# A transformer block on one core: how the high part of the row maxima is written

## The chip, the cores and the metric

The kernel runs on one core of a Trainium2 chip. The time is the device time in microseconds of one execution, and the number quoted is the median of several executions. TensorE (PE in the profile) multiplies, VectorE (DVE), ScalarE (ACT) and GpSimd (POOL) work on tiles of 128 partitions, and SyncE (SP) issues most of the transfers.

## What is computed

One block of a conditioned transformer, in fp32: two sequences of 2048 tokens, 512 channels, 16 heads of 32 channels, and an MLP of 2048 hidden channels. A condition vector gives shift, scale and gate for both halves.

```python
mod = jax.nn.silu(condition) @ Wada + bada
sh_a, sc_a, gt_a, sh_m, sc_m, gt_m = jnp.split(mod, 6, axis=1)
xm = _layernorm(x, g1, be1) * (1.0 + sc_a[:, None, :]) + sh_a[:, None, :]
x = x + gt_a[:, None, :] * _attention(xm, Wqkv, Wproj, bproj)
xm = _layernorm(x, g2, be2) * (1.0 + sc_m[:, None, :]) + sh_m[:, None, :]
h = jax.nn.gelu(xm @ W1 + b1, approximate=False)
x = x + gt_m[:, None, :] * (h @ W2 + b2)
```

The attention is causal and its softmax is over the keys:

```python
scores = jnp.einsum('bhqd,bhkd->bhqk', q, k) * scale
scores = jnp.where(causal, scores, -jnp.inf)
attn = jax.nn.softmax(scores, axis=-1)
```

The softmax needs, for every query, the largest of its scores. How these maxima are stored is what the change touches.

## The kernel before

**Stages.** Per sequence: layer norm and the products for queries, keys and values (`Qkv`), attention (`attention_phase`), the output projection (`project_phase`). The MLP of all tokens comes last. In the profiled execution the first sequence's attention runs from about 225 to 800 us, the second's from about 1060 to 1635 us.

**Units.** Attention is cut into units `(c, i)`: four heads `c` (`HC` = 4) and a block `i` of 512 queries, in four tiles of 128 (`TQ` = 4). A sequence has 16 units, in the order `i` = 0, 1, 2, 3 for the first four heads and 0, 2, 1, 3 for the others. A unit with block `i` looks at `i + 1` blocks of 512 keys.

**Every score is computed twice.** First with queries on the partitions, for the maxima only: `bank` (L424) multiplies one tile of queries by one block of keys into a PSUM bank `s` and VectorE takes the row maximum into a column of `mx`, with `tensor_reduce` (L441) for a full block and with a masked sum and maximum (L436, `junk`, followed by a read of its accumulator) for the block on the diagonal. There are two banks `s` (`ps_sp`, `bufs=2`); in some steps one of the `st` banks is borrowed. A bank can be written again only when VectorE has read it. Second with keys on the partitions (`scores_t`, L524): `st` is started with minus the maximum of each query (a matmul of `sel`, all -1, with `fold`), the scores are added to it, ScalarE takes the exponential into `e` (L565), GpSimd masks the diagonal tiles (L571) and adds pairs and fours of `e` tiles for the row sums (L593, `ee`), and TensorE multiplies `e` by the values into `o` and by ones into `sm`.

**From maxima to `fold`.** When the last maximum of a unit is there, `score` calls `split` (L444). `mx` has 16 rows of four heads times four tiles, with one value for each key block. If there is more than one block, L453 takes the maximum over the blocks into `m`, 128x16. Then two numbers are written for each maximum, next to each other in one of three tiles `mhl`: the high part, `m` written in the matmul's type fp32r (L455), and the low part, `m` less the high part (L456). Later `rows` (L492) lets TensorE transpose `mhl` into a bank `s` (`ps_m`) and VectorE spreads that into `fold` (L500).

**Order.** TensorE runs its matmuls in program order, as written. Scores for the maxima run up to two units ahead (`AHEAD` = 2) and are dealt out between the steps of the unit under work by planned costs: `cost` for a bank, `due` for what is to be done by a step. So there are stretches, at the end of a unit, in which every allowed score is already done. VectorE takes its instructions in the order of one queue: what stands behind a stalled one waits, whatever it needs. GpSimd does the same; in attention it has trains of eight or more additions `ee` of 128x512, and in the last stage of the queries and keys it prepares MLP weights (L911, `w`). The last unit's `ee` sums run on VectorE.

Of the kernel before, what the change touches and what calls it, by code (L numbers as in the profile page):

```python
# [12 lines left out]
ALU = mybir.AluOpType  # L13
AX = mybir.AxisListType
# [13 lines left out]
def dit_block_kernel(  # L28
# [35 lines left out]
    nc = tc.nc  # L64
# [5 lines left out]
    HC = P // HD  # L70
# [12 lines left out]
    def pool(name, bufs=1, **kw):  # L83
# [25 lines left out]
        axis=AX.XY,  # L109
        op=ALU.add,  # L110
# [7 lines left out]
    for n in range(AHEAD + 1):  # L118
        m = bp.tile([P, HC, HD], F32R, tag=f"mhl{n}", name=f"mhl{n}")
# [154 lines left out]
    class Row:  # L274
# [169 lines left out]
        def split(self, u, mx):  # L444
            nb = units[u][1] + 1
            hl = mhl[u % (AHEAD + 1)][:, :, : 2 * TQ].rearrange(
                "p h (t l) -> p h t l", l=2
            )
            if nb == 1:
                m = mx[:, :, 0]  # L450
            else:
                m = bp.tile([P, HC * TQ], F32, tag="m1", name="m1", bufs=2)
                nc.vector.tensor_reduce(m, mx, axis=AX.X, op=ALU.max)  # L453
            m = m.rearrange("p (h t) -> p h t", h=HC)
            nc.vector.tensor_copy(hl[:, :, :, 0], m)  # L455
            nc.vector.tensor_tensor(  # L456
                hl[:, :, :, 1], m, hl[:, :, :, 0].bitcast(F32), ALU.subtract
            )
# [670 lines left out]
    with ExitStack() as mlp:  # L1129
# [249 lines left out]
        for m in range(NM):  # L1379
            h = [  # L1380
                [
                    mp.tile([P, 4, MT], F32, tag="h4", name="h4", bufs=2 * FC // 4)
                    for _ in range(FC // 4)
                ]
                for _ in range(2)
            ]
# [87 lines left out]
```

## Time and profile before

| What | Value |
|---|---|
| Median of three executions | 2513.37 us (2510.52 to 2516.57) |
| Profiled execution, its time | 2510.99 us |
| Profiled execution, its span | 2509.3 us |
| Mean granted TensorE clock | 0.99 |
| L441, maxima of full blocks, 768 of them | 429.6 us in 634 from `s`, 92.2 us in 134 from `st` |
| L593 on GpSimd, pair sums `ee<-e` | 420.2 us in 336, 1287 ns each |
| L593 on GpSimd, four sums `ee<-ee` | 211.2 us in 168, 1285 ns each |
| L455 with `m`, units of two to four key blocks | 50.9 us in 24 |
| L455 with `mx`, units of one key block | 1.4 us in 8 |
| L453 | 4.8 us in 24 |

A row of a timeline gives start in us, duration in us, engine, line, operation, output and inputs with shapes, how many were merged, and in brackets how long the engine had been idle before and what ended that. A group's row ends with busy time, mean ns of one, and idle time before it. A matmul with another operand may start while the one before is still shown as running, since the ends of matmuls are modelled.

### The profile page before, as it was taken

What the parts mean: (1) busy time and instruction counts of PE and PEld (TensorE: products, weight loads), DVE (VectorE), ACT (ScalarE), POOL (GpSimd) and SP (SyncE); (2) the same over time, 40 slices, a digit from 0 to 9 for tenths busy, and PEclk for the clock granted to TensorE, in tenths of its full rate; (3) what the DMA queues carried; (4) which work ended last, traced back from release to release, by engine and by line L of the source; (5) the groups of instructions that cost most, each with busy time, mean ns of one, the idle gap of its engine ahead of it and who ended that gap; (6) DMA issues with size and microseconds to landing.
All of it is one profiled execution on the core that took longest, in us unless ns stands there. A gap on an engine that the chain in (4) does not pass through costs nothing.

```text
span 2509.3 us, 30950 instructions
## 1 busy us (share of the span) xinstructions
PE 2440.3 (97%) x10977; PEld 1178.9 (47%) x10977; DVE 1401.8 (56%) x2820; ACT 892.6 (36%) x1667; POOL 978.7 (39%) x1158
## 2 busy tenths in 40 slices
PE   7999999999999999999999999999999999999998
PEld 3445545445444444554554454444444444444443
DVE  3455667767666535567676766664363353344424
ACT  1213555554545012155545454613313312311310
POOL 0052786766762361068667675332101101200200
PEclk9999999999999999999999999999999999999999
DMA  6667123051224695440514113263224233332423
GB/s 223 202 218 202 46 50 87 22 110 43 87 88 144 215 302 193 133 95 22 110 43 110 27 51 118 69 226 114 88 92 140 78 101 109 109 96 70 140 84 96
DMA packets 133445, 285.71 MB, mean 114 GB/s; under 512 B 13301, under 2 KB 42525, under 8 KB 128426
## 3 DMA queue, kind: packets, MB, share of 16 engines
q1 hardware_dynamic: 126226, 257.47, 34.4%
q0 software_dynamic: 5376, 23.07, 2.6%
q10 hardware_dynamic: 1688, 3.19, 0.4%
q8 instruction: 86, 1.41, 0.2%
q14 instruction: 69, 0.57, 0.1%
HBM read 209.76 MB, written 81.79 MB: 116 GB/s over the span
## 4 chain that ended last, share of the span: by engine, by line
PE 62%; DVE 3%; DMA 1%; SPq 1%; issue 1%; ACT 0%; DVEq 0%; ACTq 0%
PE ps_h L192 15%; PE ps_y L192 15%; PE st L192 9%; PE o L192 5%; PE s L192 5%; PE ps_qk L192 4%; PE ps_o L192 3%; PE sm L192 2%; PE ps_v L192 2%; SPq L336 1%; PE ps_xt L200 1%; PE ps_o L200 0%; DMA r<-sum 0%; DMA q<-hl 0%; DVE junk L436 0%
## 5 line engine op out<-in xcount | busy, mean ns | idle before, releaser
L565 ACT ACTIVATE e<-st 128x512 f32<-128x512 f32 (+1 forms) x1152 | 572.8, 579 | 516.7 <-PE st L192 458.0
L441 DVE TENSOR_REDUCE mx<-s 128x1 f32<-128x512 f32 x634 | 429.6, 687 | 236.2 <-PE s L192 233.4
L593 POOL TENSOR_TENSOR ee<-e 128x512 f32<-128x512 f32 x336 | 420.2, 1287 | 242.8 <-ACT e L565 242.8
L192 PE MATMUL s<-kst,qst 128*128 128x512 f32 (+3 forms) x1066 | 483.4, 460 | 28.4 <-DVE mx L441 10.4
L192 PE MATMUL st<-qst,kst 128*128 128x512 f32 (+3 forms) x1280 | 405.3, 393 | 0.0
L192 PE MATMUL o<-e,vv 128*32 128x512 f32 (+3 forms) x2560 | 296.5, 545 | 0.0
L192 PEld LDWEIGHTS s<-kst,qst 128*128 128x128 f32 x1066 | 201.3, 190 | 202.3 <-DVE mx L441 80.4
L192 PE MATMUL ps_h<-sx,w 128*128 128x512 f32 x640 | 286.7, 592 | 0.0
L1245 POOL TENSOR_TENSOR c<-c 128x512 f32<-128x512 f32 x32 | 40.6, 1270 | 626.8 <-DVE c L1207 626.8
L436 DVE CUSTOM_DVE_ANT_0 junk<-s,causal 128x384 bf16<-128x384 f32 (+3 forms) x432 | 212.2, 491 | 126.9 <-PE s L192 118.2
L192 PE MATMUL ps_y<-sh,w 128*128 128x512 f32 x640 | 276.7, 592 | 0.0
L192 PEld LDWEIGHTS st<-qst,kst 128*128 128x128 f32 x1280 | 226.9, 193 | 92.8 <-issue 63.2
L192 PE MATMUL ps_qk<-xmT,wqkv 128*128 128x512 f32 x512 | 242.0, 601 | 2.2 <-DVE xmT L248 2.2
L571 POOL TENSOR_SCALAR_AFFINE_SELECT e<-e 128x128 f32<-128x128 f32 (+1 forms) x384 | 122.8, 344 | 290.2 <-ACT e L565 284.2
L1207 DVE TENSOR_TENSOR h<-c,ps_h 128x512 f32<-128x512 f32 x128 | 88.0, 688 | 232.5 <-PE ps_h L192 232.5
L593 POOL TENSOR_TENSOR ee<-ee 128x512 f32<-128x512 f32 x168 | 211.2, 1285 | 0.0
L192 PEld LDWEIGHTS ps_h<-sx,w 128*128 128x128 f32 x640 | 121.1, 190 | 150.2 <-issue 149.7
L192 PEld LDWEIGHTS ps_y<-sh,w 128*128 128x128 f32 x640 | 120.7, 190 | 147.8 <-issue 146.4
L1231 ACT ACTIVATE h<-h,cols 128x512 f32<-128x512 f32 x128 | 92.3, 721 | 182.4 <-DVE h L1207 182.4
L192 PE MATMUL st<-fold,sel 32*128 32x512 f32 (+1 forms) x1152 | 154.0, 485 | 2.3 <-DVE fold L500 2.0
L192 PEld LDWEIGHTS ps_qk<-xmT,wqkv 128*128 128x128 f32 x512 | 95.2, 192 | 98.7 <-issue 91.2
L192 PEld LDWEIGHTS st<-fold,sel 32*128 32x128 f32 x1152 | 61.2, 183 | 145.3 <-ACT e L565 75.2
(123 smaller groups left out, 2361.8 us busy)
## 6 DMA issues: line engine op xcount, KB each, us to landing
qst<-q SPq DMA_DIRECT2D x128, 256.0 KB
w<-w1d SPq DMA_DIRECT2D x34, 896.0 KB
w<-w2d SPq DMA_DIRECT2D x28, 1024.0 KB
kst<-k SPq DMA_DIRECT2D x24, 1024.0 KB
q<-hl SPq DMA_DIRECT2D x32, 512.0 KB
k<-hl SPq DMA_DIRECT2D x32, 512.0 KB
kst<-k SPq DMA_DIRECT2D x32, 256.0 KB
w<-in_L_cond_W_dram POOLq DMA_DIRECT2D x64, 128.0 KB, 4.3
```

The source lines that it names most:

```text
L192: return tc.keep_in_program_order(nc.tensor.matmul(*args, **kw))
L200: return tc.keep_in_program_order(nc.tensor.transpose(dst, src, ident[:n, :n]))
L336: nc.sync.dma_start(dst, inv_d[self.b][u].unsqueeze(1).to_broadcast([HC, HD, QB]),)
L436: nc.vector.tensor_tensor_reduce(junk[:, :w], s[:, :w], causal[:, QB - w :], 1.0, MASKED, ALU.add, ALU.max, m,)
L441: nc.vector.tensor_reduce(m, s[:, :w], axis=AX.X, op=ALU.max)
L565: act(nc.scalar.activation(e[:, :w], sts[h][:, :w], AF.Exp))
L571: nc.gpsimd.affine_select(d, d, pattern=[[0, len(tiles)], [1, P]], compare_op=ALU.is_ge, fill=0.0, base=0, channel_multiplier=-1,)
L593: act(engine.tensor_tensor(dst, x, y, ALU.add))
L1207: nc.vector.tensor_tensor(dst, x, y, op)
L1231: nc.scalar.activation(d, d, AF.Gelu, bias=col(r_b1 + chunk, 1))
L1245: nc.gpsimd.tensor_tensor(c1_, c1_, c2_, ALU.subtract)
```

## The change

The high part is no longer a copy of `m`. It is a second maximum over the key blocks of `mx`, with the same result, written straight to its places in `mhl`. `m` is still made by the first maximum, and the subtraction that gives the low part still reads `m` and the high part.

```diff
             m = m.rearrange("p (h t) -> p h t", h=HC)
-            nc.vector.tensor_copy(hl[:, :, :, 0], m)
+
+            nc.vector.tensor_reduce(
+                hl[:, :, :, 0],
+                mx.rearrange("p (h t) n -> p h t n", h=HC),
+                axis=AX.X,
+                op=ALU.max,
+            )
             nc.vector.tensor_tensor(
                 hl[:, :, :, 1], m, hl[:, :, :, 0].bitcast(F32), ALU.subtract
             )
```

## The prediction

> **What bounds the kernel now.** I read the page's busy shares, then the chain of waits.
>
> ```profile
> PE 2440.3 (97%) x10977; PEld 1178.9 (47%) x10977; DVE 1401.8 (56%) x2820; ACT 892.6 (36%) x1667; POOL 978.7 (39%) x1158
> PE 62%; DVE 3%; DMA 1%; SPq 1%; issue 1%; ACT 0%; DVEq 0%; ACTq 0%
> ```
>
> TensorE sets the end; VectorE has 3% of the chain. An edit on VectorE is worth only what TensorE now waits for it. So I went to the edited lines (the view of a source line: min/median/max ns):
>
> ```profile
> L453 DVE TENSOR_REDUCE m<-mx x24: 174/204/221, 167.2 to 1583.0; 128x16 f32<-128x32 f32 x8, 128x16 f32<-128x48 f32 x8, 128x16 f32<-128x64 f32 x8
> L455 DVE CAST mhl<-m x24: 165/563/7393, 167.4 to 1583.3; 128x16 fp32r<-128x16 f32 x24
> L456 DVE TENSOR_TENSOR mhl<-m,mhl x24: 164/210/1500, 168.7 to 1583.9; 128x16 fp32r<-128x16 f32 x24
> ```
>
> The same 16-element copy takes 0.165 or 7.393 us, the subtraction after it up to 1.5, while the maximum never leaves 0.174 to 0.221. By shape the groups give the copy 50.9 us in 24 (mean 2119 ns) and the subtraction 13.5 us (mean 560). At their unhindered 0.17 us they would cost 4.1 each, so 46.8 and 9.4 us are waiting. No semaphore explains it; GpSimd does. The timeline of the two engines around one long copy:
>
> ```profile
> 349.84 8.70 POOL L593 TENSOR_TENSOR ee<-e 128x512 f32<-128x512 f32 x7
> 358.50 1.07 POOL L571 TENSOR_SCALAR_AFFINE_SELECT e<-e 128x128 f32<-128x128 f32 x4
> ...
> 351.06 0.20 DVE L453 TENSOR_REDUCE m<-mx 128x16 f32<-128x48 f32 x1
> 351.30 7.37 DVE L455 CAST mhl<-m 128x16 fp32r<-128x16 f32 x1
> 358.70 0.21 DVE L456 TENSOR_TENSOR mhl<-m,mhl 128x16 fp32r<-128x16 f32 x1
> 364.95 0.69 DVE L441 TENSOR_REDUCE mx<-s 128x1 f32<-128x512 f32 x1 [6.04 <-PE s L192]
> ```
>
> The copy stands until GpSimd's train of additions is over; the maximum at 351.06, beside the same train, does not. But the last line is the point: VectorE then idles 6.04 us for want of scores, so this stall of 7.2 us is covered. Another place, with TensorE's rows:
>
> ```profile
> 443.64 0.22 DVE L453 TENSOR_REDUCE m<-mx 128x16 f32<-128x64 f32 x1
> 443.90 0.56 DVE L455 CAST mhl<-m 128x16 fp32r<-128x16 f32 x1
> 444.50 1.19 DVE L456 TENSOR_TENSOR mhl<-m,mhl 128x16 fp32r<-128x16 f32 x1
> 445.61 0.28 DVE L436 CUSTOM_DVE_ANT_0 junk<-s,causal 128x128 bf16<-128x128 f32 x1
> ...
> 444.50 0.42 PE L192 MATMUL st<-kst,qst 128*128 128x384 f32 x1
> 445.95 0.49 PE L192 MATMUL s<-kst,qst 128*128 128x512 f32 x1 [1.04 <-DVE mx L436]
> ...
> 748.42 0.33 PE L200 MATMUL ps_m<-ident,mhl 128*128 128x128 f32 x1 [0.32 <-DVE mhl L456]
> ```
>
> Here the waits are short (0.4 and 1.0) but uncovered: the masked maximum at 445.61 is queued behind the subtraction, holds one of the two score banks, and TensorE stops for 1.04 us.
>
> [...] the copy and the two-input subtraction stretch under GpSimd, L453 takes 0.203 us with it (351.06) and 0.204 without (225.84). [...] the copy at 351.30 missed six ends of GpSimd instructions in a row, while those at 443.90 and 295.93 got in at the next.
>
> **The change part by part.** *Replaced.* The 24 copies fall into groups (timeline of each): A, six of 7.27 to 7.39 us (units with three key blocks, like 351.30); B, four of 0.56 (443.90, 592.16, 1277.60, 1425.96), each followed by a subtraction of 1.19; C, two of 0.56 at the last units (746.57, 1583.30), followed by 1.20; D, two of 0.61 (295.93, 1129.70), followed by 0.98; E, one of 0.78 at 167.37, followed by 1.50; F, nine without GpSimd beside them, 0.17. Each becomes a maximum over 32, 48 or 64 elements: L453's row, 0.176, 0.203 and 0.220, so 8 x (0.176 + 0.203 + 0.220) = 4.8 us for 50.9. The eight copies of units with one key block (0.174 each) become maxima over one element, 16 values: about 0.17, no difference. Output stride and type of the new maximum are not in the trace; I take L453's price[...].
>
> *Moved.* The new maximum reads mx, not m, so it no longer waits for L453 and goes straight behind it. The program order on VectorE shows two more shifts: at D the subtraction comes ahead of the masked maximum of 256, at E ahead of the first of two maxima that stood around it. Other engines and all queues keep their instructions and order.
>
> *Where it shows.* A: up to 6 x 7.1 = 43 us leave VectorE and TensorE gets nothing: no TensorE gap lies beside those stalls, VectorE idles about 6 us after each. F: no wait, 0.03 each way, 0. B: the subtraction now asks at about 444.12 (443.64 + 0.22 + 0.22 + 0.04), 0.26 us before GpSimd's next instruction at 444.38. Let in there, it ends near 444.55 instead of 445.69 and the masked maximum starts 1.1 us earlier; TensorE's gaps before that s matmul are 1.04, 1.02, 1.04 and 1.02 (timeline, four places): 4.1 us. Its next gaps (0.38 and 0.41 at 447.70 and 448.41) come from VectorE's unbroken queue, so they move along and stay. C: the transpose of mhl waits 0.32 and 0.34 us for the subtraction: 0.65 us, after which the value products before it are last. E: the gap of 0.44 us at 170.38 follows the 1.50 us subtraction: 0.44 us if it now goes in at 168.03. D: VectorE gains 0.8, but TensorE has no gap there, 0. Sum 4.1 + 0.65 + 0.44 = 5.2 us.
>
> Bounds of the unknown, the subtraction's luck: if it misses its end at B and C it ends exactly where it ends today (445.69), 0; if all goes well and the shift also swallows the 0.4 us gaps at B, 4 x 0.8 more, 8.4. I take 5.2: of thirteen two-input operations that had to wait for GpSimd in the trace, twelve got in at the next end (L456 eight times at B, C and D; L974 at 814.49, 1645.96, 1650.49 and 1667.40), and the one at 168.66 missed two.
>
> **Base.** The profiled execution took 2510.99 us (span 2509.3); 5.2 less is 2505.8. The median of the three runs is 2513.37, 2.4 above it, so the forecast is 2508.2 us.
>
> **The rivals.**
> 1. *The wait moves whole to the subtraction.* It inherits the copy's delay[...]. For: 1.50 at 168.66. Against: [...] at B it already gets in after one instruction. At A that is covered, at B it ends at 445.69 as now: 2513, within 2.
> 2. *Slower: the subtraction starves at D and E.* There it is now ahead of maxima that free score banks. At D it asks near 296.1, in a train of additions that lasts to 300.16. Up to one instruction's wait (296.45) is free; from the second on (297.68) the masked maximum of 256, today at 296.45, is 1.2 us late and so is the s matmul behind its bank; to the end of the train, 3.7. Two places at 3.7 and E at 2.0 (168.06 to 170.07) make +9.4; with B gaining nothing 2522.8, at 1.2 each about 2516. For: the six copies of A missed every end. Against: at 296.80 the subtraction, in this very train, got in after one.
> 3. *The change doesn't do what it says:* [...] Then every wait stays: 2513. Against: L453's even 0.174 to 0.221.
>
> **How the numbers follow.** No difference can be told below about 0.2% (5.0 us). Likeliest case 0.68, own range 2504 to 2511; as its 5.2 lies at the bound, but most of what I left out (the 0.4 us gaps at B) adds to it, I put 0.56 of it on faster by over 0.2% and 0.12 on less. Rivals 1 and 3: 0.15 and 0.05, both within. Rival 2: 0.12, slower. So 0.56, 0.32, 0.12. The range: down to the 8.4 (2505) and 2 more for TensorE's granted clock (in 1422 to 1438 it was 0.79 instead of 1.00, 3.4 us), so 2503; up past rivals 1 and 3 to 2514.5.
>
> **What would show it.** After: the new maximum at 0.17 to 0.22 in all 24; VectorE's total down by 40 us or more; subtractions at B under 0.5 us and no gap of 1.0 before the s matmul; no gap before the transposes of C. Wrong, if subtractions of 1.2 us remain at B, if some of 7 us appear at A (harmless), or if a gap on TensorE appears after 296 or 1130.

## The result, and the profile after

| What | Before | After |
|---|---|---|
| Median, measured side by side | 2515.04 us of 5 (2510.52 to 2521.73) | 2503.07 us of 5 (2499.64 to 2505.15) |
| Ratio, 95% interval | 1 | 0.9957 (0.9938 to 0.9976) |
| Profiled execution: time, span | 2510.99, 2509.3 us | 2505.15, 2503.4 us |
| Maximum or copy for the high part, units of two to four key blocks | 50.9 us in 24 | 4.8 us in 24, at most 0.213 each |
| Subtraction, the same units | 13.5 us in 24 | 53.1 us in 24 |

By the ratio the kernel is faster by 0.4%, about 11 us; the two medians lie 12.0 us apart. A gain of 5.2 us, to 2508.2, had been forecast, with 2503 to 2514.5 as the range: 2503.07 is just inside its lower end. First the busy times and the chain of waits of the kernel after (the page):

```profile
PE 2437.2 (97%) x10977; PEld 1176.0 (47%) x10977; DVE 1396.0 (56%) x2820; ACT 892.5 (36%) x1667; POOL 979.2 (39%) x1158
PE 62%; DVE 2%; DMA 1%; SPq 1%; issue 1%; ACT 0%; DVEq 0%; ACTq 0%
```

VectorE lost only 5.8 us of busy time (1401.8 to 1396.0), not 40. Where the rest went stands in the view of a source line (min/median/max ns, first and last start), here the new maximum and the subtraction of the kernel after:

```profile
L456 DVE TENSOR_REDUCE mhl<-mx x32: 161/186/213, 116.9 to 1577.1; 128x16 fp32r<-128x16 f32 x8, 128x16 fp32r<-128x32 f32 x8, 128x16 fp32r<-128x48 f32 x8, 128x16 fp32r<-128x64 f32 x8
L462 DVE TENSOR_TENSOR mhl<-m,mhl x24: 166/436/7255, 166.2 to 1577.4; 128x16 fp32r<-128x16 f32 x24
```

The new maximum never waits. The longest subtraction, at most 1.5 us before, now takes 7.255: at the six units of group A it inherits the copy's stall whole (7.19 to 7.26 us), and VectorE still idles afterwards. The first of the six in the timeline of the kernel after (VectorE):

```profile
352.46 0.19 DVE L456 TENSOR_REDUCE mhl<-mx 128x16 fp32r<-128x48 f32 x1
352.69 7.24 DVE L462 TENSOR_TENSOR mhl<-m,mhl 128x16 fp32r<-128x16 f32 x1
366.22 0.69 DVE L441 TENSOR_REDUCE mx<-s 128x1 f32<-128x512 f32 x1 [6.29 <-PE s L192]
```

The four places of group B went otherwise. The timeline of the kernel after around the first of them, VectorE and then TensorE, and last the place of group C, with the value products, the transpose of `mhl` and the matmuls behind it:

```profile
444.83 0.22 DVE L453 TENSOR_REDUCE m<-mx 128x16 f32<-128x64 f32 x1
444.97 0.21 DVE L456 TENSOR_REDUCE mhl<-mx 128x16 fp32r<-128x64 f32 x1
445.21 0.45 DVE L462 TENSOR_TENSOR mhl<-m,mhl 128x16 fp32r<-128x16 f32 x1
445.58 0.28 DVE L436 CUSTOM_DVE_ANT_0 junk<-s,causal 128x128 bf16<-128x128 f32 x1
...
445.68 0.43 PE L192 MATMUL st<-kst,qst 128*128 128x384 f32 x1
445.95 0.47 PE L192 MATMUL s<-kst,qst 128*128 128x512 f32 x1
...
744.29 1.07 PE L192 MATMUL o<-e,vv 128*32 128x512 f32 x8
745.28 0.33 PE L200 MATMUL ps_m<-ident,mhl 128*128 128x128 f32 x1
745.54 0.82 PE L192 MATMUL st<-fold,sel 32*128 32x512 f32 x4
```

The subtraction gets in after 0.45 us instead of 1.19. The masked maximum starts 0.75 us after L453 (445.58 less 444.83), where it was 1.97 before (445.61 less 443.64), and the `s` matmul follows the `st` matmul with no bracket behind its row: the gap of 1.04 us is gone, here and at the other three places. The transpose no longer waits 0.32 us either, but the four matmuls behind it now take 0.82 us. In the kernel before they took 0.51 (its timeline, TensorE):

```profile
748.68 0.51 PE L192 MATMUL st<-fold,sel 32*128 32x512 f32 x4
```

So most of the wait at C has moved on by one step. Group D went well at one place (1129.31: 0.52 us) and badly at the other. Its timeline, GpSimd, VectorE and TensorE:

```profile
291.25 6.24 POOL L599 TENSOR_TENSOR ee<-e 128x512 f32<-128x512 f32 x5
297.41 0.32 POOL L577 TENSOR_SCALAR_AFFINE_SELECT e<-e 128x128 f32<-128x128 f32 x1
...
293.32 4.44 DVE L462 TENSOR_TENSOR mhl<-m,mhl 128x16 fp32r<-128x16 f32 x1
297.68 0.41 DVE L436 CUSTOM_DVE_ANT_0 junk<-s,causal 128x256 bf16<-128x256 f32 x1
...
295.24 0.50 PE L192 MATMUL st<-qst,kst 128*128 128x512 f32 x1
298.16 0.63 PE L192 MATMUL s<-kst,qst 128*128 128x512 f32 x1 [2.42 <-DVE mx L436]
```

The subtraction asks at 293.32, misses the end of every addition, and ends with the first masking instruction behind them (297.41 plus 0.32 us). The masked maximum of 256 behind it is late, and TensorE stands for 2.42 us. That is the second rival's mechanism, at one of its places.

Every kernel here runs the same 10977 matmuls in the same order, so the same matmul's start can be compared between two traces: the change of that difference across a place is what the place cost or gave. Counted as gain from before to after, it is 0.7 us at E, a loss of 4.0 at the first D, and a gain of 1.17 to 1.22 at each of the four B. At the two C it is 0.1 each, and at the six A it stays within 0.03 us of nothing. Behind the fourth B another 3.03 us are gained: there TensorE's granted clock was 0.50 from 1431.0 to 1437.8 in the kernel before, and 1.00 in the kernel after. No term of the prediction's sum had priced that.

### The profile page after: what moved, and what is told of

The parts are those of the page before. It is cut to its first block, busy times and chain, and to the rows that moved or that the text cites. A ratio compares the mean times of both kernels' runs of the same rounds, so it can differ in the third digit from the quotient of the medians.

```text
span 2503.4 us, 30950 instructions
## 1 busy us (share of the span) xinstructions
PE 2437.2 (97%) x10977; PEld 1176.0 (47%) x10977; DVE 1396.0 (56%) x2820; ACT 892.5 (36%) x1667; POOL 979.2 (39%) x1158
## 4 chain that ended last, share of the span: by engine, by line
PE 62%; DVE 2%; DMA 1%; SPq 1%; issue 1%; ACT 0%; DVEq 0%; ACTq 0%
PE ps_h L192 15%; PE ps_y L192 15%; PE st L192 9%; PE o L192 5%; PE s L192 5%; PE ps_qk L192 4%; PE ps_o L192 3%; PE sm L192 2%; PE ps_v L192 2%; SPq L336 1%; PE ps_xt L200 1%; PE ps_o L200 0%; DMA r<-sum 0%; DMA q<-hl 0%; DVE junk L436 0%
```

## The experiments

Ratios are to the kernel before on the same chip, with 95% intervals. There are three sets, each on a chip of its own: before once more, the maximum over one element, four blocks only and the kernel of reductions alone; then the change again, reductions alone again, three blocks only and the first gap; then the rest. Questions: does the gain come from the operation (the maximum is not held up beside GpSimd, the copy is) or from dropping the wait for the first maximum? Which units bring it? Does a TensorE gap cost its length, or more, by a clock that falls behind it? And is D a loss by the change? Theory 'port' of the expectations says that the copy and the subtraction wait for GpSimd, that a maximum does not, and that only the waits that TensorE feels count. Its name is an assumption on the cause, which no run here shows.

**The kernel before once more.** No edit.

> The kernel before, unchanged, in a second profile. Theory 'port' ([...] only the waits that TensorE feels count): ratio 1.000 within 0.2%; six copies near 7.3 us again at the units with three key blocks, about 1.04 us of idle TensorE at the four places of group B; whether a copy or a subtraction at the two places of group D (near 296 and 1130 us) misses several ends of GpSimd instructions is luck, and would show as a TensorE gap of 2 us or more there. Theory 'clock' (a good part of the gain is that TensorE's half-clock spells happened to be shorter): the half-clock time of this profile differs from the 52.8 us of the first one by 10 us or more, with the same program.

Ratio 1.0013 (0.9998 to 1.0029). In this execution the copies of the kernel before were late at both places of D, and two of its four B gaps had a spell, that is a stretch of half clock, behind them. All its spells together last 53.0 us, as good as the 52.8 us of the first profile, so the difference of 10 us or more that theory 'clock' forecast did not come. Timeline of this run at the first D and at the second B (VectorE, then TensorE):

```profile
294.39 4.58 DVE L455 CAST mhl<-m 128x16 fp32r<-128x16 f32 x1
...
595.41 0.42 PE L192 MATMUL st<-kst,qst 128*128 128x384 f32 x1
596.85 0.50 PE L192 MATMUL s<-kst,qst 128*128 128x512 f32 x1 [1.02 <-DVE mx L436]
```

And the windows behind that gap (length in us, busy time and count of PE, PEld, DVE, ACT and POOL, granted clock, DMA share, GB/s):

```profile
596.90:599.80 2.90, 2.12 (x12) 0.70 (x12) 2.58 (x9) 0.00 (x0) 2.90 (x5) 1.00 0.02 6
599.80:606.60 6.80, 6.80 (x26) 4.16 (x27) 2.49 (x12) 2.33 (x4) 3.22 (x7) 0.50 0.01 2
606.60:613.40 6.80, 6.45 (x42) 3.53 (x42) 4.58 (x16) 2.46 (x7) 2.24 (x5) 1.00 0.43 99
```

Three microseconds after a gap of 1.02 us the clock is halved for 6.80 us: TensorE is busy throughout and passes 26 matmuls, against 42 in the next 6.80 us. So being late at D isn't new with the change (of the three profiles of before only the first has neither late), and spells come and go from one execution to the next.

**A maximum over one element instead of the copy.** It still waits for `m`, as the copy did.

```diff
-                mx.rearrange("p (h t) n -> p h t n", h=HC),
+                m.unsqueeze(3),
```

> The high part is a maximum over one element of m: still a read of m behind the wait for the first maximum, like the copy[...]. Theory 'port': 0.17 to 0.22 us in all 32, TensorE's gaps of 1.04 us at group B gone, ratio to before like the change, 0.994 to 0.998. Theory 'wait' (the gain came from no longer waiting for the first maximum): nothing gained, ratio 1.000.

Ratio 0.9974 (0.9963 to 0.9985). Source view of this run, the high part and the subtraction:

```profile
L456 DVE TENSOR_REDUCE mhl<-m x24: 159/170/173, 166.8 to 1579.1; 128x16 fp32r<-128x16 f32 x24
L462 DVE TENSOR_TENSOR mhl<-m,mhl x24: 165/353/7130, 167.6 to 1579.3; 128x16 fp32r<-128x16 f32 x24
```

Same input, same output, same wait as the copy, and 0.173 us at most where the copy took up to 7.393. The B gaps are gone; at D the second place was late (4.22 us, TensorE gap 2.32). Some two thirds of the change's gain are here without the second maximum over the blocks, and the intervals of the two, measured on different chips, overlap. By the starts each B gains 1.2 us as with the change: it is the operation that counts there, not the wait for `m`, and theory 'wait' has fallen. That GpSimd holds the copy is read from the ends: all 146 copies and subtractions of more than 0.3 us in the fourteen profiles of this text ended within 0.13 us after the end of a GpSimd instruction. No run took GpSimd's work away.

**Four key blocks only, three key blocks only.** The new maximum in some units, the copy in the others.

```diff
+            if nb == 4:   # the other run: nb == 3
+                nc.vector.tensor_reduce(...)
+            else:
+                nc.vector.tensor_copy(hl[:, :, :, 0], m)
```

> The change at the eight units with four key blocks alone (groups B, C and D); the other 24 keep the copy. Theory 'port': the six copies of 7.3 us at three key blocks stay and cost nothing, B gives 4 x 1.2 us and C about 0.5, D stays a matter of luck (0 to 4 us lost at each place); ratio 0.996 to 0.999, profile 4 to 6 us below that of before where D goes well. Theory 'long copies' (the 43 us of long stalls matter after all): ratio 1.000.

> The change at the eight units with three key blocks alone. The six copies of 7.3 us go (their subtraction waits 7.1 us instead), B, C, D and E stay as before. Theory 'port, only uncovered waits count': ratio 1.000 within 0.15%, though the longest stalls of all are the ones edited. Theory 'long copies': 0.997.

Four: 0.9972 (0.9961 to 0.9982). The eight units of B, C and D bring about two thirds of the change's ratio alone, with the copies of A left in (five of 7.3 to 7.8 us, one of 14.7); D went well at both places (0.48 and 0.50 us). Three: 0.9993 (0.9982 to 1.0003), no difference. Source view of the run with three blocks only, the subtraction:

```profile
L465 DVE TENSOR_TENSOR mhl<-m,mhl x24: 164/1192/8021, 166.3 to 1587.6; 128x16 fp32r<-128x16 f32 x24
```

The longest stalls of the kernel were edited there, and they only moved to the next instruction (7.2 to 8.0 us), under the same idle time. By the starts the six places of A cost and gave nothing, within 0.01 us. Its B gaps stayed at 1.01 to 1.04 us.

**Reductions alone.** The low part becomes a sum over two neighbouring values, the maximum and its negated high part, so that the subtraction goes too. All four instructions are one-input reductions.

```diff
...
+            pr = bp.tile([P, HC * TQ, 2], F32, tag="m1", name="m1", bufs=2)
+            nc.vector.tensor_reduce(pr[:, :, 0], mx, axis=AX.X, op=ALU.max)
+            nc.vector.tensor_reduce(
+                pr[:, :, 1].bitcast(F32R), mx, axis=AX.X, op=ALU.max, negate=True
+            )
...
-            nc.vector.tensor_tensor(
-                hl[:, :, :, 1], m, hl[:, :, :, 0].bitcast(F32), ALU.subtract
-            )
+            with nc.allow_low_precision(reason="two terms"):
+                nc.vector.tensor_reduce(
+                    hl[:, :, :, 1],
+                    pr.rearrange("p (h t) n -> p h t n", h=HC),
+                    axis=AX.X,
+                    op=ALU.add,
+                )
```

> The subtraction goes as well: m and the negated high part are written side by side and added by a tensor_reduce over the pair, so that all four instructions are maxima or sums with one input. Theory 'port': every one of them at 0.16 to 0.23 us, none of 7 us; no TensorE gap after 295 or 1130 us; 0 to 5 us below the change, ratio to before 0.993 to 0.996, and the smallest spread of all. Rival 'VectorE work' (two more small instructions at each unit, about 0.3 us, stand in the queue at B): 4 x 0.3 = 1.2 us lost again, ratio 0.996 to 0.998.

Ratio 0.9959 (0.9946 to 0.9971), at the upper end of what theory 'port' forecast. By the starts B gains 1.2 us at each place here too, so the two more instructions of rival 'VectorE work' took nothing back. Source view of this run, the high and the low part:

```profile
L454 DVE TENSOR_REDUCE mhl<-mx x32: 159/184/210, 117.7 to 1571.7; 128x16 fp32r<-128x16 f32 x8, 128x16 fp32r<-128x32 f32 x8, 128x16 fp32r<-128x48 f32 x8, 128x16 fp32r<-128x64 f32 x8
L461 DVE TENSOR_REDUCE mhl<-m x32: 174/182/188, 117.8 to 1571.8; 128x16 fp32r<-128x32 f32 x32
```

None of these instructions stalls, and at D (timeline, TensorE) the `s` matmul that stood for 2.42 us in the kernel after follows at once:

```profile
296.79 0.50 PE L192 MATMUL st<-qst,kst 128*128 128x512 f32 x1
297.12 0.39 PE L192 MATMUL s<-kst,qst 128*128 128x512 f32 x1
```

**The change and reductions alone, on one chip.** No edits. The first expectation measures the change against reductions alone.

> The change once more, beside the others on one chip. The new maxima and the subtractions at B and C behave as in its first profile; at D the subtraction either gets in after one GpSimd instruction (about 0.5 us) or after four (about 4.4 us), and where it is four, TensorE has a gap of 2 to 2.5 us. Theory 'port': ratio to before 0.995 to 0.998, and 0 to 0.15% above the kernel [...].

> [...] Theory 'port': 0.9945 to 0.9972 of before, below or level with the change on the same chip, no TensorE gap above 0.95 us in attention apart from those at 225 and 1060 us that all kernels have.

The change 0.9962 (0.9949 to 0.9976), reductions alone 0.9950 (0.9938 to 0.9963). In its profile the change was late at both places of D; by the comparison of starts against the version of reductions alone they cost 4.0 us each, 2.4 of it gap and the rest behind it. The version of reductions alone was late at neither. Its expectation of no TensorE gap above 0.95 us did not hold: gaps of 2.8 and 3.7 us stand near 713 and 1550 us, as in every kernel here. The intervals overlap, so which of the two is faster isn't settled by this pair.

**A gap of 1 us put back.** In the kernel of reductions alone the first maximum reads every block 24 times in the four-block units other than the first four heads', which is 1.75 us instead of 0.22.

```diff
+            if nb == 4 and units[u][0] > 0:
+                nc.vector.tensor_reduce(
+                    pr[:, :, 0],
+                    mx.unsqueeze(2).to_broadcast([P, HC * TQ, 24, nb]),
+                    axis=AX.XY,
+                    op=ALU.max,
+                )
...
```

> [...] with one VectorE instruction lengthened at the four places of B and the two of C (the first maximum runs over 24 repeats of mx, 1536 elements instead of 64, same result, about 1.5 us longer), so that the queue there is as late as it was with the copy and the subtraction. Theory 'gap and clock' (a TensorE gap of 1 us at B costs its length, and sometimes a spell of half clock behind it, as at 1431 in the first profile of before and at 599.8 and 1289.3 in the second): 8 to 10 us above the kernel without it, and half-clock spells behind some of the four gaps. Theory 'gap alone': 4 x 1.25 + 2 x 0.35 = 5.7 us above it, no such spells.

> The kernel with a TensorE gap of about 1.07 us put in at the four places of B, a second profile and more executions. In the profiles so far a spell of half clock began within 5 us behind 4 of 16 such gaps, and behind none of 24 where the gap was gone. Theory 'gap and clock': 0 to 2 spells behind the four, time 6 to 10 us above the kernel without the gaps. Theory 'gap alone': none, 5.5 us above it.

Ratios 0.9970 (0.9961 to 0.9980) and 0.9977 (0.9965 to 0.9990), against 0.9950 and 0.9939 for reductions alone on the same chips: 5 and 9.5 us. Timeline of the first of the two, VectorE and TensorE:

```profile
440.71 1.75 DVE L451 TENSOR_REDUCE m<-mx 128x16 f32<-128x1536 f32 x1
...
443.07 0.49 PE L192 MATMUL s<-kst,qst 128*128 128x512 f32 x1 [1.07 <-DVE mx L436]
```

The delay reproduces the gap of B (1.07 to 1.08 us at all four) with no GpSimd in it. By the starts of the same matmuls a place of B cost 1.5 us and one of C 0.1, except the fourth B of the second run: a spell of 6.8 us followed there, and it cost 4.4. So the first run, with no spell and 5 us, fits theory 'gap alone' and misses the 8 to 10 us of the other; the second, with one spell in four and 9.5 us, fits 'gap and clock'.

**The gap doubled.** The first maximum reads every block 48 times, which is 3.35 us.

> The same with the first maximum over 48 repeats (3072 elements, about 3.35 us instead of 1.75), so that TensorE stands about 2.7 us at each of the four places of B and about 1.9 at C. Theory 'gap and clock': gaps of 2.4 us at D had a half-clock spell behind them in all eight cases, so four spells of 3.4 or 6.8 us here, and the time lies 4 x (3.1 + 1.7 to 3.4) plus 2 x 1.9, or 23 to 30 us, above the kernel without gaps. Theory 'gap alone': no more spells than before, 4 x 3.1 + 2 x 1.9 = 16 us above it.

Ratio 1.0075 (1.0059 to 1.0091). Timeline of this run (TensorE) at the first B, and then windows before and behind the gap there (columns as above):

```profile
445.30 0.79 PE L192 MATMUL s<-kst,qst 128*128 128x512 f32 x1 [2.68 <-DVE mx L436]
```

```profile
438.40:442.60 4.20, 4.20 (x24) 1.94 (x22) 3.79 (x6) 2.42 (x6) 4.20 (x4) 1.00 0.00 0
445.30:455.50 10.20, 9.39 (x36) 4.95 (x36) 5.15 (x19) 2.32 (x4) 3.82 (x7) 0.50 0.01 2
```

All four gaps are 2.68 us and each has a spell of half clock at its end or 2.1 us behind it, of 6.8 or 10.2 us: in 10.20 us TensorE passes 36 matmuls, while 4.20 us at full clock passed 24. The gaps alone are 10.7 us; against reductions alone on the same chip (0.9939) this one loses 34 us, more than the 23 to 30 that theory 'gap and clock' forecast. By the starts, the four places cost 5.8 to 7.0 each, 26.5 together; the two places of C, with gaps of 1.97 and 1.98 us and a spell of 3.4 us behind each, cost 2.8 each on top. For gaps of 2 us and more, that a gap costs its length alone has fallen.

**Reductions alone and before, a third time.**

> [...] 0.994 to 0.997 of before, no half-clock spell behind the places of B and D.

> The kernel before in a third profile, to count: half-clock spells behind the four gaps of B (1 and 2 of 4 so far in its two profiles) and late copies at D (0 and 2 of 2). Theory 'gap and clock': at least one spell behind B, and behind each late copy at D. Theory 'gap alone': spells fall anywhere. Time level with before.

0.9939 (0.9924 to 0.9954) and 0.9996 (0.9981 to 1.0010). Before was again late at both places of D (gaps 2.37 and 2.42) and had one spell behind a B gap; the version of reductions alone had neither.

Over the thirteen profiles of before, after and the experiments other than the doubled gap, counted by what stood at the place:

| Place | Profiles | Spells of half clock within about 5 us behind it |
|---|---|---|
| B with its gap of 1.0 to 1.1 us | before three times, three blocks only, gap put back twice | 6 of 24 |
| B without the gap | after twice, reductions alone three times, copy by maximum, four blocks only | 0 of 28 |
| D with a gap of 2.3 to 2.4 us | before three times and three blocks only (6 gaps), after twice and copy by maximum (4 gaps) | 10 of 10 |

Late at D were 6 of 8 with the copy in the way (before three times, three blocks only) and 4 of 8 with only the subtraction (after twice, copy by maximum, four blocks only).

Which of the short gaps get a spell can be read from the same traces. In each profile the spells start on one grid, in the first profile of before, for example, at 229.5, 717.6, 823.4 and 1065.7 us, which are 143, 31 and 71 steps of 3.413 us apart. The spells of each of the fourteen profiles fit such a grid within 0.04 us. Of the 24 short gaps, the six with a spell began 2.86 to 3.18 us into a step or 0.03 us into the next; the eighteen without began 0.41 to 2.67 us into one. This was found afterwards, and no run set it on purpose.

The mean granted clock of every execution is on record. The span times one less this clock estimates the time that the slow clock took (from above, since TensorE can also idle under it); the rest is time at full clock. The means have standard errors of 0.5 to 1.7 us for the slow clock and 0.3 to 0.9 us for the rest:

| Set | Kernel | Executions | Slow clock, us | Rest, us |
|---|---|---|---|---|
| first | before | 61 | 21.5 | 2487.7 |
| first | copy by maximum | 22 | 21.1 | 2482.2 |
| first | four blocks only | 22 | 19.0 | 2483.0 |
| first | reductions alone | 16 | 19.8 | 2479.6 |
| second | before | 26 | 23.6 | 2490.7 |
| second | the change | 6 | 21.7 | 2483.6 |
| second | reductions alone | 5 | 21.5 | 2479.6 |
| second | gap put back | 13 | 21.4 | 2485.4 |
| third | before | 25 | 23.6 | 2487.2 |
| third | reductions alone | 6 | 18.3 | 2478.5 |
| third | gap put back | 12 | 21.1 | 2484.9 |
| third | gap doubled | 6 | 42.2 | 2488.7 |

In the second set the change gains 7.1 us at full clock and 1.9 by the clock (though the rest of the kernel before is 3 us higher there than in the other sets). The doubled gap loses 24 us by the clock. The gap of 1 us loses 5.8 and 6.4 us at full clock; by the clock it loses nothing in the second set and 2.8 us in the third.

## Why the prediction was right, and where not

*The bound and the operation.* Right. TensorE's waits decided, VectorE's 40 us of waiting stayed and cost nothing, and the new maximum does not wait beside GpSimd (third rival fallen: 0.161 to 0.213 us in all 32). The maximum over one element shows by itself that it is the operation: 0.159 to 0.173 us, where the copy of the same values took 0.165 to 7.393. And in the kernel after, beside the same train of additions, the maximum L456 took 0.19 us at 352.46 and the two-input L462 behind it 7.24. Why GpSimd holds up the one and not the other, no run shows.

*A, at nothing.* The price of 0 was right: with three blocks only, 0.9993, and nothing at the six places by the starts. The picture behind it was wrong. "up to 6 x 7.1 = 43 us leave VectorE" did not happen; as the first rival had it, the subtraction inherited the stall. The prediction reasoned from twelve of thirteen two-input operations that got in at the next end, and the six copies that missed every end were the better model at A. Nor is A free always: in 3 of the 48 places of A in the eight profiles that have a copy or a subtraction there, the stall lasted 14.6 us or more, and TensorE lost 1.0 to 1.2 us by the starts.

*B, 4.1 us.* The mechanism was right at all four places; the term was too small. First, each place gave 1.2 us rather than the gap's 1.01 to 1.04. Second, the term priced a gap at its length. Of the 16 gaps that the stretched copy and subtraction made in four profiles, 5 had a spell of half clock behind them, and one of 6.8 us cost 3.0; that is 5/16 x 4 x 3.0 = 3.8 us per execution, an estimate from few places. The clocks of all executions give less: 1.9 us with a standard error of 1.7 for the change, all its places together. The prediction had put the spell at 1431 into the range only, as a wobble of the clock. That spells belong to the gap is shown for the doubled gap, by its time and by four spells in four; for the gap of 1 us it rests on the counts (6 of 24 against 0 of 28) and on the grid, and the times of the gap put back don't settle it.

*C and E, 0.65 and 0.44.* The waits before the transposes of C are gone, but the term is wrong: by the starts each place gave 0.1 us, 0.2 in all, since the matmuls behind the transpose took up the rest. What holds those was not tested. E gave 0.70 in both profiles of the change, but in the four profiles with the old instructions at E (before twice more, three and four blocks only) it moved between a gain of 0.39 and a loss of 0.35 by itself, so little of it is shown.

*D, 0.* Wrong as a fact and nearly right as a sum. The subtraction does starve there, as the second rival said, at about 4.0 us a time. But the kernel before pays the same, and rather more often (6 of 8 against 4 of 8). The profile that the prediction was made from had neither. With 2 places x (6/8 - 4/8) x 4.0 this is some 2.0 us for the change, an estimate from eight places each; the counts are too few to say that the difference is real.

By the counts these are 4.8 + 3.8 + 0.2 + 0.7 + 2.0 = 11.5 us; the two measurements of the change gave 10.8 and 9.6 (0.9957 and 0.9962 of 2513.37), about twice the forecast 5.2. The 1.9 us by the clock are less than the counts of B and D say, so the split between B, the spells and D is an estimate. That the median lies within the range, by 0.07 us, is partly luck: the range's lower end came from the 0.4 us gaps at B, which stayed, and from 2 us for the clock.

When a request gets in follows how far into a GpSimd addition it comes. In the eight profiles that have copies or subtractions beside additions of 128x512, the copies that came 0.73 to 0.78 us into one got in at its end (26 of 26), and those that came 0.17 to 0.69 us into one missed it (30 of 30); at D they came at 0.73 in the first profile of before and at 0.67 to 0.69 in the later ones. A subtraction that was the first to ask got in where it came 0.85 to 0.97 us into an addition (25 of 25) and missed at 0.24 to 0.49 (24 of 24); between 0.81 and 0.82 it went both ways, as did the two that came within 0.06 us of an addition's start. A subtraction right behind a copy that had got in, at 0.10 to 0.35 us, always got in at the next end (26 of 26). Eight of the twelve cases on which the prediction built its odds were of this last kind. Why it is so stays open, and no run set this on purpose.

The best version seen is the one of reductions alone: 0.9959, 0.9950 and 0.9939, the smallest ratio within each of its three sets. In no profile did it have a gap at B or D. Its lead over the change, 0.0012 on the same chip, is within the intervals.

## What to carry to other kernels

When a small VectorE instruction takes 0.17 us in one place and 7 in another, look at what GpSimd runs beside it, and rewrite it, rather than move it, as an operation that a trace shows at its short time beside the same work (here a `tensor_reduce` of 16 to 64 elements, at most 0.22 us); but take out every instruction of the chain that stretches there, since the next one inherits the wait (7.2 us at A). Price it only where TensorE stands for it, and look there at what the matmuls behind will wait for next. A gap can also cost more than its length, since a spell of half clock can follow it (one of 6.8 us cost 3.0 us here). Before a rare event is counted for or against a change, look how often it comes in several profiles of the same kernel.

## What the runs showed of the hardware

TensorE's granted clock fell from 1.00 to 0.50 behind gaps of 1.0 to 2.7 us, which the prediction had not reckoned with. Gaps of 2.3 to 2.7 us at B and D had half clock at their end or behind them 14 of 14 times, the two of 2.0 us at C also, and the gaps of 1.0 to 1.1 us at B 6 of 24 times. The gaps of 0.8 us before an `s` matmul that waits for `fold`, six in the attention of each profile, had none in 84. The spells in attention lasted 3.4, 6.8 or 10.2 us.

No bound on a VectorE instruction's wait for GpSimd shows in these traces: a subtraction of 16 elements took 14.6 us in the second run of the change, a copy 14.7 with four blocks only, and a copy and its subtraction 8.1 and 6.6 in the second profile of before. All three were at units of three key blocks, and there TensorE felt it (gaps of 0.73, 0.97 and 0.75 us). The reductions of 16 to 64 elements took 0.159 to 0.222 us in the source views of five kernels (before, after, the maximum over one element, four blocks only and reductions alone).
